# Attention with a gated output on one core: where a weight copy stands in ScalarE's order, and when placements and late fetches are issued

## Chip, core and metric

The kernel runs on one core of a Trainium2 chip. The metric is device time in microseconds of one execution. A core has five engines that run side by side, each through its own instructions in order: TensorE (PE, matmuls; PEld is its weight load), VectorE (DVE), ScalarE (ACT), GpSimd (POOL) and SyncE (SP). SP computes nothing here; it issues nearly all DMA transfers, one after the other, and a transfer that has to wait for something holds up all that stand behind it in SP's order. ScalarE and VectorE are in the same position: an instruction that waits holds those behind it.

## What is computed

The input x is (2, 1024, 512), all in float32. Cut to what matters:

```
xn = layernorm(x)
q, k, v = xn @ Wq.T + bq, xn @ Wk.T + bk, xn @ Wv.T + bv     # 32 heads of 16
s  = causal_softmax(q k^T / 4) v @ Wo.T + bo
g  = silu(xn @ W_base.T + b_base + routed_low_rank(xn))      # 8 experts, best 2
out = x + s * g
```

## The kernel before, in words

The 1024 tokens of a batch are two chunks of 512 (`c` is 0 or 1), the 32 heads four column blocks of 8 heads (`oc` is 0 to 3). A unit `(b, oc, c)` is the attention of one column block for one chunk of queries. `units` fixes the order of all units (line 466), `plan` cuts each into steps (line 1231). A step computes scores of some keys against the queries on PE (`scores`, line 1524, into two PSUM tiles `s`), takes the exponential of both on ScalarE (tiles `pt`, line 56 is the helper through which all VectorE and most ScalarE instructions are recorded), masks on GpSimd (line 1566), and multiplies with the values on PE one step later (`values`, line 1571, into `av`). The scores of a step need the two PSUM tiles back from the exponentials of the step before.

Into these steps all other work is filled (`fill`, line 1431), in an order that is fixed when the program is written, by a planner's own account of the engines: `act.free` and `ve.free` are the times at which ScalarE and VectorE are reckoned to be done, `begins` is when the next step starts. Three kinds of things are filled in. Tasks with a cost are PE work, cut to share the steps evenly. Tasks without a cost (layernorm, routing, weight sums) are run step by step on VectorE; they pause at a `WAIT` till the next step, and stop where `enough()` says that VectorE is late. `later` is a list of single pieces with the step from which they may be issued; a piece that has an entry in `costs` is put off while ScalarE is not `calm`, up to a last step. `urgent` is a list of DMA pieces that `place_urgent` (line 1519) issues: at the end of the tasks' turn in `fill`, and ahead of each step's scores.

Projections are done in seven block products in place of eight (sums of blocks of the weights and of the tokens are formed on VectorE first; `PARTS` names the seven). For the query and key columns of block `oc`, `qk_weights_task` (line 621) loads 0.5 MB of columns (`load_qk`, line 123), has ScalarE copy them so that the heads of a pair lie side by side (`pair_up`, line 129), forms four sums on VectorE, and stores the 1 MB result to HBM for the second batch (line 642), which fetches it again (line 626). Two buffers `wqk` serve all blocks. Blocks 0 and 1 are prepared elsewhere; the task's copy serves blocks 2 and 3. The weights of values, gate and output come in parts of 256 KB (`issue_parts`, line 617), four parts ahead of their use; those that are sums are read back from a stored copy `kept`.

A finished query or key block is split into high and low parts, and half of its rows are moved to other partitions by DMA before scores can use them: `place_keys` (line 465), `place_queries` (line 484, tile `qT`, 512 KB in two transfers). `split` puts them on the `urgent` list.

The output stage of a chunk (`out_task`, line 877) computes four blocks in the order (0,0), (1,1), (0,1), (1,0). For each, VectorE multiplies with the gate block `gr` and adds the input block `xr`, both fetched from HBM (lines 890 and 892) into two buffers each: the first two pairs are fetched at the start, the third and the fourth after (0,0) and (1,1) are done with theirs. The result is stored by line 903.

The attention's denominators go out by DMA (`den`, `dens`), are inverted, and come back (`back`, then `avs<-back`, line 1050).

Of the kernel before, what the change touches and what calls it, by code (L numbers as in the profile page):

```python
# [81 lines left out]
def direct(ctx, tc, sound, x, wq, wk, wv, wo, wb, wa, wg, wB, bq, bk, bv, bo, bb, out):  # L82
# [35 lines left out]
    def load_qk(oc):  # L118


        t = sb.tile([P, 4 * KC, P], F32, tag="wqk", bufs=2, name=f"wqk{oc}")
        for n, src in enumerate((wq, wk)):
            nc.sync.dma_start(
                out=t[:, (2 + n) * KC : (3 + n) * KC],
                in_=src.rearrange("(kc p) o -> p kc o", p=P)[:, :, oc * P : oc * P + P],
            )
        return t

    def pair_up(t):


        raw, paired = (
            t[:, i * KC : (i + 2) * KC].rearrange("p k o -> p (k o)") for i in (2, 0)
        )
        act.copy(
            paired.rearrange("p (g r a) -> p g a r", a=2, r=HD),
            raw.rearrange("p (g a r) -> p g a r", a=2, r=HD),
        )
# [15 lines left out]
    wqks = [load_qk(0)]  # L154
# [62 lines left out]
    WAIT = object()  # L217
    PAUSE = object()
    turned_at, now = {}, [0]
# [351 lines left out]
    def four_sums(at, to):  # L571

        ve.tensor_tensor(to[1], at[0, 1], at[0, 0], ALU.subtract)
        yield PAUSE
        ve.tensor_tensor(to[3], at[1, 1], at[0, 1], ALU.subtract)
        yield PAUSE
        ve.tensor_tensor(to[2], at[1, 1], to[1], ALU.subtract)
        yield PAUSE
        ve.tensor_tensor(to[4], at[1, 0], to[2], ALU.subtract)
# [41 lines left out]
    def qk_weights_task(n):  # L621

        oc = n % KC
        if n >= KC:
            wqks.append(sb.tile([P, 4 * KC, P], F32, tag="wqk", bufs=2, name=f"wqk{oc}"))
            nc.sync.dma_start(out=wqks[n], in_=qk_kept[oc])
        else:
            if n >= 2:
                wqks.append(load_qk(oc))
                for _ in range(3):  # L630
                    yield WAIT
                pair_up(wqks[n])
                yield WAIT
            w = wqks[n]
            yield from four_sums(
                {(i, j): w[:, 4 * j + 2 * i : 4 * j + 2 * i + 2] for i in range(2) for j in range(2)},
                {t: w[:, 2 * KC + 2 * t - 2 : 2 * KC + 2 * t] for t in range(1, 5)},
            )
            qk_kept[oc] = dram.tile([P, 4 * KC, P], F32, tag=f"kept_qk{oc}", bufs=1, name="kept")
            qk_ready[n] = now[0]  # L640
            yield WAIT
            nc.sync.dma_start(out=qk_kept[oc], in_=w)
            for _ in range(2):
                yield WAIT
        qk_ready.setdefault(n, now[0] + 2)
        yield WAIT
# [229 lines left out]
    def out_task(k):  # L876

        _, b, c = stages[k]
        y, g = block_of(chunk_tile(b, c)), block_of(g_tiles[b, c])
        order = [(0, 0), (1, 1), (0, 1), (1, 0)]  # L880
        xts, gts = {}, {}

        def block(t, i, j):
            rows = slice(c * C + BK * i, c * C + BK * i + BK)
            return t[b, rows, BK * j : BK * j + BK].rearrange("(t p) o -> p t o", p=P)

        def load():
            i, j = order[len(xts)]
            xts[i, j] = sb.tile([P, 2, BK], F32, tag="xr", name=f"xr_{b}_{c}_{i}{j}")
            nc.sync.dma_start(out=xts[i, j], in_=block(x, i, j))  # L890
            gts[i, j] = sb.tile([P, 2, BK], F32, tag="gr", name=f"gr_{b}_{c}_{i}{j}")
            nc.sync.dma_start(out=gts[i, j], in_=g(i, j))

        def final(i, j):
            def gated():
                ve.scalar_tensor_tensor(y(i, j), y(i, j), 0.5, gts[i, j], ALU.mult, ALU.mult)
                ve.tensor_tensor(y(i, j), y(i, j), xts[i, j], ALU.add)
                later.append((now[0] + 2, store))
                if i == j:
                    later.append((now[0] + 2 - i, load))  # L900

            def store():
                nc.sync.dma_start(out=block(out, i, j), in_=y(i, j))

            patient.append(gated)
            later.append((now[0], gated))

        load()
        load()
        yield from block_task(k, y, final)  # L910

    g_tiles = {}
# [175 lines left out]
    turns, turned, posts, posted, later, patient, last_out = [], [], {}, [], [], [], []  # L1088
# [16 lines left out]
    bases, whole_wo, splits, costs, urgent = {}, [], [], {}, []  # L1105
# [200 lines left out]
    for b in range(NB):  # L1306
        for c in range(NC):
# [69 lines left out]
            else:  # L1377
                before = starts[b, KC - 1, c] + 2
                Task(len(plan) - 7, bases_task(b, c), 0.0, after=before - 12, takes={"xnT": 2})
                n = len(units) - 3  # L1380
# [50 lines left out]
    def fill(n):  # L1431


        nonlocal spent
        now[0], begun_at = n, spent
        within = 0 <= n < len(plan)
        for x in tasks:
            x.waiting = False
        for turn in [turn for turn in turns if turn[0] <= n]:
            turns.remove(turn)  # L1440
            turn[1]()

        begin = len(plan) - 3
        even = (total - spent) / max(1, len(plan) - n)
        if n == len(plan) - 1:
            even = MM
        if n >= starts[units[-1]] - 8 and n < begin:
            even = sum(x.left for x in tasks if x.steps.__name__ not in ("whole_task", "rest_task"))
            even /= begin - n
        elif n < begin:  # L1450
            even = min(even, (total - last_work - spent) / (begin - n))
        share = spent + even
        if n >= 5:

            left = 0.0
            for x in tasks:
                if x.steps.__name__ in ("whole_task", "rest_task"):
                    continue
                left += x.left
                if x.due > n:  # L1460
                    share = max(share, spent + left / (x.due - n))
        while True:
            free = [x for x in tasks if x.cost and x.released(n)]
            if not free or free[0].due > n + 1:
                due = [x.steps.__name__ for x in tasks if x.cost and x.due <= n + 1]
                if due:
                    assert late, (n, due)
                    turn_late()
                    continue
                if not free or spent + (MM / 2 if n < 12 else MM / 8) >= share:  # L1470
                    break
            task = active[0] if active else free[0]
            active[:] = [task]
            ve.ready = act.ready = clock[0] + SV + spent - begun_at + MM
            cost = task.step()
            if cost is None or cost is WAIT:
                task.waiting = True
                active.clear()
            else:
                spent += cost  # L1480
        ve.ready = act.ready = 0.0
        begins = clock[0] + max(2.3, SV + spent - begun_at)
        enough = lambda more=0.65: late_by(n + 1, begins, more) > 0
        calm = lambda more: act.free + more < begins + 0.75
        for x in [x for x in splits if x[0] <= n]:
            if room["qT"] and room["kT"] and (calm(1.1) or n >= starts[x[2]] - 5):
                splits.remove(x)
                room["qT"] -= 1
                room["kT"] -= 1
                x[1]()  # L1490
        for x in [x for x in later if x[0] <= n]:
            if x not in later or x[0] == n and x[1] in patient and enough():
                continue
            if x[1] in costs and not calm(costs[x[1]][0]) and n < costs[x[1]][1]:
                continue
            later.remove(x)
            x[1]()
        for x in [x for x in tasks if not x.cost]:
            if not x.released(n):
                continue  # L1500
            said = PAUSE
            while said is not None and said is not WAIT:
                if x.due > n and enough(1.85 if x.due > n + 20 else 0.65):
                    break
                said = x.step()
            x.waiting = said is WAIT
        clock[0] = begins
        place_urgent(n)
        issue_parts()
        for _ in range(1 if active or len(plan) - 5 < n < len(plan) else 2):  # L1510
            if late and (min(x[0] for x in late) <= n or not within):
                turn_late()
# [6 lines left out]
    def place_urgent(n):  # L1519
        for x in [x for x in urgent if x[0] <= n]:  # L1520
            urgent.remove(x)
            x[1]()
# [124 lines left out]
    while late or turns or tasks:  # L1647
        fill(last + 99)
# [462 lines left out]
```

## Time and profile before

| what | value |
|---|---|
| median of 4 runs | 560.43 us (560.03 to 561.37) |
| the profiled execution, its time | 560.81 us |
| its span, first to last instruction | 559.0 us |
| mean granted TensorE clock | 0.994 |
| PE busy | 540.7 us of the span |
| ScalarE busy | 351.0 us |
| VectorE busy | 334.7 us |
| GpSimd busy | 118.5 us |
| share of the 16 DMA engines that the SP transfers took | 42.8% |
| longest total wait of SP: for PE to free a weight part (line 617) | 81.1 us in 35 waits |

How to read it: all times in a profile are of one execution, counted from the start of its span. A bracket behind an instruction gives the idle time of its engine just before it and what ended that time. PE at 97% means that nearly every other engine's idle time is free of cost; what counts is idle time of PE, and stretches in which the granted clock is below 1. The clock is the share of full speed at which PE was allowed to run. Time between a transfer's issue on SP and the instruction that waited for it is the transfer's latency; the DMA columns of a window tell how busy the 16 engines were with all transfers together.

### The profile page before, as it was taken

How to read it: one execution, taken by the hardware profiler on the slowest of the kernel's cores; microseconds unless marked ns; L12 is line 12 of the kernel's file. 1: busy time of each engine (PE TensorE's matmuls, PEld its weight loads, DVE VectorE, ACT ScalarE, POOL GpSimd, SP SyncE). 2: the span in 40 equal slices, each digit the busy share in tenths (PEclk: the TensorE clock that was granted, in tenths of full speed). 3: DMA queues.
4: the chain of work that ended last, by engine and by line, in shares of the span. 5: the costliest groups of instructions: out<-in, count | busy, mean ns of one | idle time of the engine just before them, and what ended most of it. 6: DMA issues, size and time to landing. Idle time of an engine off the chain costs nothing.

```text
span 559.0 us, 19432 instructions
## 1 busy us (share of the span) xinstructions
PE 540.7 (97%) x8411; PEld 280.1 (50%) x8411; DVE 334.7 (60%) x693; ACT 351.0 (63%) x389; POOL 118.5 (21%) x248
## 2 busy tenths in 40 slices
PE   8999999779999999999999999999999999999994
PEld 8435444444445554454645554444545554456651
DVE  4435587265478676466559765575267553648833
ACT  2537754655677766766667756656667777776540
POOL 2213401020213431130214330130103331020500
PEclk9999999998999999999999999999999999999998
DMA  8634370685624663732555545640124221652211
GB/s 262 173 112 172 119 232 1 211 301 179 168 77 137 226 221 113 233 112 73 185 167 174 175 155 161 205 153 23 58 80 137 79 83 45 227 171 81 97 40 45
DMA packets 65197, 79.15 MB, mean 142 GB/s; under 512 B 9560, under 2 KB 52576, under 8 KB 63696
## 3 DMA queue, kind: packets, MB, share of 16 engines
q1 hardware_dynamic: 65088, 77.83, 42.8%
q8 instruction: 68, 1.11, 0.9%
q14 instruction: 25, 0.20, 0.1%
q10 hardware_dynamic: 16, 0.00, 0.0%
HBM read 46.39 MB, written 19.37 MB: 118 GB/s over the span
## 4 chain that ended last, share of the span: by engine, by line
PE 89%; DVE 4%; DMA 3%; ACT 2%; issue 1%; SPq 0%; POOL 0%; ACTq 0%; POOLq 0%; DVEq 0%
PE av L1590 24%; PE p L228 22%; PE s L1538 17%; PE q L228 13%; PE pv L228 2%; PE po L228 2%; PE ph L228 2%; ACT pt L56 2%; PE pq L228 1%; PE pk L228 1%; DMA qT<-qT 1%; PE warm L183 1%; DVE x L56 1%; DMA wqk<-in_wk_dram 1%; DMA gr<-kept_g 1%
## 5 line engine op out<-in xcount | busy, mean ns | idle before, releaser
L56 ACT ACTIVATE pt<-s 128x1024 f32<-128x1024 f32 x288 | 290.0, 1024 | 157.0 <-PE s L1538 149.5
L1566 POOL TENSOR_SCALAR_AFFINE_SELECT pt<-pt 128x256 f32<-128x256 f32 (+1 forms) x224 | 110.5, 508 | 414.6 <-ACT pt L56 413.8
L1590 PE MATMUL av<-pt,v 128*32 128x512 f32 (+3 forms) x1680 | 156.9, 467 | 0.2 <-DVE v L56 0.2
L1538 PE MATMUL s<-qT,kT 32*128 32x512 f32 (+3 forms) x1616 | 108.8, 364 | 6.6 <-ACT pt L56 3.6
L1538 PEld LDWEIGHTS s<-qT,kT 32*128 32x128 f32 x1616 | 62.3, 183 | 65.9 <-issue 34.9
L1590 PEld LDWEIGHTS av<-pt,v 128*32 128x32 f32 x1680 | 41.6, 108 | 54.7 <-issue 38.6
L228 PE MATMUL p<-wt,asum 128*32 128x256 f32 x960 | 60.3, 387 | 0.0
L228 PE MATMUL q<-asum,wqk 128*32 128x256 f32 x832 | 51.2, 379 | 1.1 <-DVE qf L56 1.1
L228 PEld LDWEIGHTS p<-wt,asum 128*32 128x32 f32 x960 | 32.0, 112 | 29.7 <-issue 12.9
L228 PE MATMUL q<-xnT,wqk 128*32 128x256 f32 x624 | 39.5, 379 | 0.0
L228 PEld LDWEIGHTS q<-asum,wqk 128*32 128x32 f32 x832 | 26.5, 110 | 25.5 <-issue 7.2
L228 PEld LDWEIGHTS q<-xnT,wqk 128*32 128x32 f32 x624 | 20.2, 110 | 18.5 <-issue 6.6
L56 DVE TENSOR_TENSOR g<-p,g 128x512 f32<-128x512 f32 x20 | 13.8, 690 | 24.8 <-PE p L228 24.7
L56 DVE SCALAR_TENSOR_TENSOR kf<-q,kf 128x256 f32<-128x256 f32 x39 | 16.5, 424 | 19.5 <-PE q L228 18.6
L228 PE MATMUL p<-w,xnT 128*32 128x256 f32 x448 | 28.1, 379 | 0.0
L228 PEld LDWEIGHTS p<-w,xnT 128*32 128x32 f32 x448 | 15.7, 110 | 10.3 <-issue 3.6
L228 PE MATMUL p<-w,asum 128*32 128x256 f32 x320 | 20.7, 379 | 0.0
L56 DVE TENSOR_TENSOR kf<-kf,kT 128x512 f32<-128x512 f32 x15 | 10.3, 685 | 11.9 <-ACT kT L56 11.8
L228 PEld LDWEIGHTS ph<-wag_sb,xnT 128*32 128x32 f32 x512 | 15.2, 110 | 3.9 <-issue 3.3
L228 PE MATMUL po<-wo,oT 128*32 128x512 f32 x128 | 16.5, 593 | 0.4 <-ACT oT L56 0.4
L228 PE MATMUL ph<-wag_sb,xnT 128*32 128x136 f32 x512 | 16.6, 279 | 0.0
L56 DVE TENSOR_TENSOR v<-p,v 128x512 f32<-128x512 f32 x15 | 10.3, 684 | 10.5 <-PE p L228 10.4
(145 smaller groups left out, 557.8 us busy)
## 6 DMA issues: line engine op xcount, KB each, us to landing
wt<-kept SPq DMA_DIRECT2D x40, 256.0 KB
qT<-qT SPq DMA_DIRECT2D x30, 256.0 KB
x<-in_x_dram SPq DMA_DIRECT2D x16, 256.0 KB
kept<-wqk SPq DMA_DIRECT2D x4, 1024.0 KB
wqk<-kept SPq DMA_DIRECT2D x4, 1024.0 KB
kT<-kf SPq DMA_DIRECT2D x30, 128.0 KB
scr<-sq SPq DMA_DIRECT2D x6, 512.0 KB
xnT<-scr SPq DMA_DIRECT2D x24, 128.0 KB
```

Of the source, the lines that this page charges most:

```text
L56: return getattr(self.engine, name)(*args, **named)
L183: nc.tensor.matmul(warm[:, n % 4 * P : n % 4 * P + P], lhsT=ident, rhs=ident, start=True, stop=True)
L228: nc.tensor.matmul(o[j : j + 32], lhsT=lhsT[:, j : j + 32] if len(lhsT.shape) == 2 else lhsT[:, j // 32], rhs=rhs, start=start, stop=stop,)
L1538: nc.tensor.matmul(ss[s // 2][:, s % 2, col : col + w], lhsT=keys[rows, kt % TT * P : kt % TT * P + P], rhs=q[rows, halves * par + half_, ...
L1566: nc.gpsimd.affine_select(out=d, in_=d, compare_op=ALU.is_ge, fill=0.0, base=0, pattern=[[0, d.shape[1]], [1, P]], channel_multiplier=-1,)
L1590: nc.tensor.matmul(avs_now[par][32 * s : 32 * s + 32, q0 : q0 + w], lhsT=vs[b, kt][:, h * VS - HD * par : h * VS - HD * par + HP], rhs=pt[ ...
```

## The change

Three edits; the arithmetic and the number of instructions stay the same.

1. The pairing copy of blocks 2 and 3 is no longer issued by the task itself, three steps after the load. It becomes a piece of `later`, with a cost of 1.05 us of ScalarE: from the next step on it is issued when ScalarE is reckoned to have that much room, and at the latest four steps on. The task waits until it has been issued, and one step more, before it forms the sums.
2. In `fill`, `place_urgent` is called ahead of the tasks without a cost instead of behind them.
3. In the output stage, the late fetch is issued a step after its block in both cases (before: two steps after (0,0), one after (1,1)), and the multiplication of block (1,0) may be issued only from the next step.

```
@@ qk_weights_task
-                pair_up(wqks[n])
+                paired = lambda: pair_up(wqks[n])
+                costs[paired] = (1.05, now[0] + 4)
+                later.append((now[0] + 1, paired))
+                while any(x[1] is paired for x in later):
+                    yield WAIT
                 yield WAIT
@@ out_task, final
                 if i == j:
-                    later.append((now[0] + 2 - i, load))
+                    later.append((now[0] + 1, load))
...
             patient.append(gated)
-            later.append((now[0], gated))
+            later.append((now[0] + i * (1 - j), gated))
@@ fill
             later.remove(x)
             x[1]()
+        place_urgent(n)
         for x in [x for x in tasks if not x.cost]:
...
         clock[0] = begins
-        place_urgent(n)
         issue_parts()
```

Because the planner's account decides where pieces stand, the edits move more than they name. In the instruction lists of the two programs: on ScalarE the copy of block 2 moves to where the copy of block 3 stood, that one 16 instructions on, and a copy of the remainder of a query block moves ahead of two exponentials; on VectorE both groups of weight sums move later, as do the statistics, normalizing and transposes of the second batch's first layernorm and its token sums, and in two output stages token sums now stand ahead of a gated multiplication; on SP the load of block 3 and both stores of sums move later, placements of keys and queries stand ahead of them, the second transposed half of that layernorm is stored and read back later, and the late fetches of all three output stages stand ahead of stores and weight parts that they followed before. On PE and GpSimd only the cuts between neighbouring pieces of work differ.

More of the change, by code (lines that the diff above doesn't have):

```diff
@@ L631, in qk_weights_task @@
                     yield WAIT
-                pair_up(wqks[n])
+                paired = lambda: pair_up(wqks[n])
+                costs[paired] = (1.05, now[0] + 4)
+                later.append((now[0] + 1, paired))
+                while any(x[1] is paired for x in later):
+                    yield WAIT
                 yield WAIT
@@ L899, in gated @@
                 if i == j:
-                    later.append((now[0] + 2 - i, load))
+                    later.append((now[0] + 1, load))
             def store():
@@ L905, in final @@
             patient.append(gated)
-            later.append((now[0], gated))
+            later.append((now[0] + i * (1 - j), gated))
         load()
@@ L1497, in fill @@
             x[1]()
+        place_urgent(n)
         for x in [x for x in tasks if not x.cost]:
@@ L1507, in fill @@
         clock[0] = begins
-        place_urgent(n)
         issue_parts()
```

## The prediction

> **What bounds the kernel now.** I began with the page: its busy times, its slices, its chain.
>
> ```profile
> PE 540.7 (97%) x8411; PEld 280.1 (50%) x8411; DVE 334.7 (60%) x693; ACT 351.0 (63%) x389; POOL 118.5 (21%) x248
> ...
> PEclk9999999998999999999999999999999999999998
> ...
> PE 89%; DVE 4%; DMA 3%; ACT 2%; issue 1%; SPq 0%; POOL 0%; ACTq 0%; POOLq 0%; DVEq 0%
> ```
>
> TensorE is busy 540.7 of 559.0 us, so everything that any edit can win lies in 18.3 us of idle PE and in the one slice where the clock fell. The table of 10 us windows says where these are. Some 2.4 us stand ahead of 50 us and 8.3 us about the last matmuls, and the change touches neither. What is left is 0.60 + 3.08 + 2.83 between 90 and 130 us, 0.49 in 370 to 380 and 0.61 in 490 to 500.
>
> ```profile
> core 0: us, PE busy (x) PEld busy (x) DVE busy (x) ACT busy (x) POOL busy (x), PEclk, DMA share, GB/s
> ...
> 100.00:110.00 10.00, 6.92 (x140) 4.12 (x136) 0.69 (x1) 6.40 (x10) 0.00 (x0) 1.00 0.75 236
> 110.00:120.00 10.00, 10.00 (x172) 5.36 (x172) 5.47 (x12) 5.74 (x7) 2.86 (x6) 1.00 0.78 281
> 120.00:130.00 10.00, 7.17 (x92) 3.31 (x88) 7.84 (x26) 5.24 (x8) 1.27 (x2) 0.83 0.61 224
> ```
>
> The timeline of that stretch names the causes (columns: start, duration, engine, line, operation; in brackets the idle time before it and who ended it).
>
> ```profile
> 103.60 1.11 ACT L56 COPY wqk<-wqk 128x1024 f32<-128x1024 f32 x1 [3.77 <-DMA wqk<-in_wk_dram]
> ...
> 105.67 0.50 PE L1538 MATMUL s<-qT,kT 32*128 32x512 f32 x2 [2.66 <-ACT pt L56]
> ...
> 113.64 0.89 SPq L617 DMA_DIRECT2D wt<-kept  x2
> 114.58 0.46 SPq L123 DMA_DIRECT2D wqk<-in_wq_dram  x1
> ...
> 115.09 0.51 SPq L123 DMA_DIRECT2D wqk<-in_wk_dram  x1
> ...
> 115.64 1.16 SPq L465 DMA_DIRECT2D kT<-kf  x2
> ...
> 116.90 0.53 SPq L642 DMA_DIRECT2D kept<-wqk  x1
> ...
> 117.47 1.93 SPq L484 DMA_DIRECT2D qT<-qT  x2
> ...
> 124.03 0.73 PE L1538 MATMUL s<-qT,kT 32*128 32x512 f32 x8 [2.83 <-DMA qT<-qT]
> ```
>
> Two stalls follow each other. In the first, ScalarE comes to the pairing copy at 99.83 and stands there 3.77 us, because the columns (issued 98.62) land at 103.5; the exponentials queued behind it start at 104.61, so the next scores start at 105.67. In the second, the doubled queries qT are issued at 117.47, behind the next columns' load (0.5 MB) and the sums' store (1 MB), and land 6.42 us later at 123.89; the DMA engines are full from 115 to 125 us. In 1 us windows the granted clock is then 0.72, 0.50, 0.50, 0.57 from 125 to 129: 0.28 + 0.50 + 0.50 + 0.43 = 1.7 us more lost.
>
> **The change, part by part.** The instruction lists of the two programs, which hold no times, show what moves.
>
> *Pairing copy.* No instruction is added. The first copy (1.11 us) moves behind 14 ScalarE instructions, to the place where the second stood; the second (1.17 us) moves behind 16, to about 140 us. Neither then waits for its load: the first's columns have been there for 12 us. Removed: the 3.77 us stand at 99.83, and the 2.10 us one that the second copy had at 117.4. Without the first, the exponentials start 0.85 us after their scores (96.82 after 95.97 is the usual step), so 100.27 to 102.3, and PE goes on at 103.0 when its `ph` products end. The scores' following `av` stands at 107.24 now and would stand at 103.67: **3.57 us sooner**. ScalarE does not stall it again: two `hl` copies, keys (1.08) and exponentials (1.95) end at 106.3, PE wants the bank at 106.46.
>
> *What is late next.* SP doesn't move with PE here. From 98.62 to 113.64 it is held by its own order and by DMA: `back` lands at 108.5, the gate weights' 1 MB store at 113.59, and only then the two `wt` loads are issued, in both programs. PE now uses the first `wt` at 116.75 without waiting; 3.57 us sooner it asks at 113.18, and must wait. When does it land? Not after 116.75, as nothing waited then. Not before 115.9: the first bytes after the pause moved in the half microsecond from 114.5, and 256 KB at the 300 GB/s of that window take 0.85 us. I take the middle, **116.35**. So PE idles 3.2 us at a new place, and of the 3.57 us only 0.4 is left there (bounds 0 and 0.85). VectorE is no tighter: it frees the bank that this product needs at 113.7 (shuffle at 110.97, then 0.75 + 0.69 + 0.68 + 0.69, less overlap).
>
> *Placements.* After the two `wt`, SP's list now has kT, then qT at once; the load of the fourth columns comes four DMAs later, the sums' store ten. qT's issue moves from 117.47 to 113.64 + 0.89 + 1.16 + gaps = 115.72. The four column sums (1.97 us of VectorE ahead of qT's subtraction at 114.25) go too, so the ScalarE copy that SP waits for ends at 113.7 and holds nobody. Landing of qT: at least 115.72 + 2.35 = 118.1 (the small `avs<-back` took 2.35 from first issue); at most 115.72 + 6.42 = 122.14. A lone qT pair, issued at 163.95, had moved all its bytes by 167.0; here `wt` and kT (0.77 MB) are ahead and 1.5 MB less than before. I take 119.9. PE asks for it 4.45 us after the first `wt` product (116.75 to 121.20 now), at 116.35 + 4.45 = **120.8**, so it no longer waits. Gain over the whole stretch: 124.03 - 120.8 = **3.2 us**; bounds 2.8 (the `wt` at 116.75) and 3.9 (qT at 120), and 1.9 if qT keeps its 6.42.
>
> *The clock.* The row: after 2.83 us of idle PE it halved for 3.4 us, after 2.66 + 0.42 it did not. The new gap is 3.2 us, longer than either, so I leave the 1.7 us in the sum at its old price; the bounds are 0 and 1.7 us of gain. The Trainium skill, "TensorE: Matmul & The Clock Gate", section "HAM oscillation", warns of idle gaps above about 3.4 us, with a window that runs freely. By that rule neither old gap should have throttled, which the 2.83 us one did here; taken literally the new gap would escape and the estimate be 1.7 us lower.
>
> *Moved sums, loads, stores.* The first sums move to where the second stood (122.98, product at 145.3), the second to about 147 (product at 162.3); VectorE idles 2.11 us before the add at 149.66, which takes 1.74. Cost 0, hidden by 14 us or more. If that cover failed, one product would wait for up to 1.7 us. The 1 MB store lands behind `avs<-back` with no reader until the second batch.
>
> *Layernorm of the second batch.* VectorE's account shifts it later. Its last transposed tile was issued at 207.78; now it stands behind `avs<-back` (213.38 + 1.10): store 214.5, 3.1 to 4.0 us until the read may start (194.30 to 197.38, 203.79 to 207.78), 2.65 for four issues, some 2 for landing: 223.4 in the old times. Its first product is at 224.80. Cost 0, but only 1.4 us of cover.
>
> *Output stage.* The fetch of the third pair comes a step (3.4 us) sooner, ahead of a store and a weight load on SP, and the token sums stand ahead of the gated multiplication that waited for it.
>
> ```profile
> 373.04 0.69 DVE L56 SCALAR_TENSOR_TENSOR x<-x,gr 128x512 f32<-128x512 f32 x1 [2.16 <-DMA gr<-kept_g]
> ...
> 376.40 1.93 PE L228 MATMUL q<-asum,wqk 128*32 128x256 f32 x32 [0.49 <-DVE qf L56]
> ```
>
> That 0.49 us goes. The same edit in the other two output stages meets a PE without idle time: 0. Their weight load, now behind 0.5 MB, has three more tiles loaded ahead of it.
>
> **Sum.** 3.2 + 0.5 = 3.7 us off the profiled execution: 560.81 - 3.7 = 557.1 (span 559.0 to 555.3). The median of the four runs, 560.43, lies 0.38 lower, so I forecast **556.7**.
>
> **Rivals**, as times on that median.
> A. As above, the stalls merge into one at `wt` and the clock still dips once: 556.0 to 557.4. Chance 0.48.
> B. The clock stays up after the new gap: 556.7 - 1.7 = 555.0, to 554.4 if `wt` lands early. For: one old gap of 3.08 us did no harm. Against: the new one is longer and unbroken. 0.24.
> C. qT is late all the same: landing at 122.14 leaves 1.9 + 0.5 = 2.4, so 558.0, up to 559.2 if `wt` also holds. For: 6.42 us is the only latency seen here. Against: 1.5 MB fewer ahead of it. 0.12.
> D. The edits do not do what they say, or the gain is spent: VectorE adds the gate's product at 119.7 (0.68), then does the moved sums (1.74), the routing (2.05, as from 124.64 to 126.7 now) and the copy (0.68) that frees the `av` bank at 124.9; PE asks for it at 120.8 + 0.73 + 1.0 + 1.73 + 0.67 = 124.9. A slip of 3 us there leaves 559.3 to 561.6. 0.09.
> E. Slower: the layernorm's last tile. Each microsecond that it lands after 224.8 costs one, and it decides from 4.8 + 1.4 = 6.2 us beyond my reckoning. The longest waits of SP are of that size (6.2 us for VectorE, 4.2 for `back`); both in a row would cost 10.4 - 1.4 = 9.0 and give 565.7. Against: none of them stood there before. 0.07.
>
> **How the numbers follow.** A measurement of this kernel can tell about 0.2% (1.1 us) from no change, so "faster" is below 559.3: A, B and C, 0.84. D is the same, 0.09; E slower, 0.07. The range takes in A, B and C, 554.4 to 559.2.
>
> **What would show it.** Right: ScalarE's wait for `wqk` gone; PE without idle near 103 to 106 and with some 3 us before the first `p<-wt` near 113 to 116, put down to `wt<-kept`; SP issuing `wt` at 113.6 as before and qT near 115.7; scores after it near 120.8; no idle near 376. Wrong: SP's `wt` issue moved, qT still ended PE's wait, a PE gap near 220, or a `wt` that lands well before 115.9, which would make more of the 3.57 us real.

## The result, and the profile after

| | before | after |
|---|---|---|
| median | 560.28 us (78 runs) | 558.65 us (52 runs) |
| lowest to highest | 558.79 to 567.2 us | 554.68 to 561.68 us |
| span of the profiled execution | 559.0 us | 557.4 us |
| its mean granted clock | 0.994 | 0.990 |

The changed kernel is faster: ratio 0.9968, 95% interval 0.9959 to 0.9976, which is 1.8 us. The forecast was 556.7 us in a range of 554.4 to 559.2. The sign is right and the range holds the time, but the gain is half of the 3.7 us that were reckoned, and nearly all of it comes from another edit than the one that was to bring it.

First the page of the changed kernel: busy times, the granted clock in 40 slices, the shares of the chain of waits.

```profile
PE 540.8 (97%) x8411; PEld 280.6 (50%) x8411; DVE 333.0 (60%) x693; ACT 351.5 (63%) x389; POOL 116.2 (21%) x248
...
PEclk9999999979999999999999999999999999999998
...
PE 91%; DVE 2%; DMA 2%; ACT 1%; SPq 1%; issue 0%; POOL 0%; ACTq 0%; POOLq 0%; DVEq 0%
```

VectorE's share of the chain fell, and the clock has one deeper slice (7 in place of 8), still near 120 us. The 10 us windows show the same stretch.

```profile
100.00:110.00 10.00, 10.00 (x188) 5.61 (x192) 0.87 (x2) 8.62 (x12) 0.63 (x2) 1.00 0.77 239
110.00:120.00 10.00, 5.37 (x82) 2.57 (x72) 4.53 (x14) 3.60 (x5) 1.71 (x5) 0.81 0.57 217
120.00:130.00 10.00, 9.85 (x143) 4.89 (x140) 5.52 (x20) 5.32 (x6) 1.27 (x2) 0.84 0.60 183
```

PE's 3.08 us idle at the copy are gone (10.00 busy in 100 to 110) and so are the 2.83 us at qT. In their place stand 4.63 us between 110 and 120, and the clock is below 1 in two of these 10 us windows in place of one. PE is busy 25.22 us of these 30, before 24.09, in part only because it works longer at the lower clock. The timeline names the new wait.

```profile
104.19 0.93 SPq L1037 DMA_DIRECT2D back<-rc  x1
110.63 1.04 SPq L1054 DMA_DIRECT2D avs<-back  x2
111.77 0.39 SPq L597 DMA_DIRECT2D kept<-w_gate  x1
115.68 0.89 SPq L617 DMA_DIRECT2D wt<-kept  x2
...
117.87 1.23 SPq L484 DMA_DIRECT2D qT<-qT  x2
...
118.52 1.93 PE L228 MATMUL p<-wt,asum 128*32 128x256 f32 x16 [4.63 <-DMA wt<-kept]
...
125.02 0.74 PE L1542 MATMUL s<-qT,kT 32*128 32x512 f32 x8
```

The chain of waits (start, length, what) runs through three transfers:

```profile
104.19 6.39 DMA back<-rc
...
111.77 3.90 DMA kept<-w_gate
115.68 2.71 DMA wt<-kept
```

These transfers, 13 us in all, follow one upon the other: `back` must land before SP comes to `avs<-back`, that one stands ahead of the gate sums' store on SP, and the fetch of `wt` reads what that store wrote. PE arrives 3.5 us sooner at the end of a chain that does not arrive sooner.

Two stretches of PE hold the whole gain. The first runs from SP's load of block 2's columns (near 99 us) to the first `h` product (near 135), the second from the first `ph` product after 262 us to the first after 385. Each number is of one profiled execution.

| kernel | first stretch, us | second stretch, us |
|---|---|---|
| before | 37.16 | 124.55 |
| copy_alone | 35.97 | 124.21 |
| output_alone | 35.19 | 122.99 |
| output_gated_alone | 35.70 | 123.00 |
| output_fetch_alone | 36.15 | 124.27 |
| after | 36.22 | 123.02 |
| keep_warm | 36.96 | 122.99 |
| gate_store_first | 33.08 | 122.99 |
| gate_store_no_copy | 33.29 | 123.00 |
| columns_store_later | 31.83 | 122.98 |
| both_stores_moved | 29.92 | 122.99 |
| both_stores_no_copy | 36.57 | 123.02 |

From before to after the first stretch gives 0.94 us, the second 1.53; between them 0.36 is lost, and the start was 0.47 later in this execution: with 0.04 at the end that is the 1.6 us of the two spans. The second column splits cleanly by whether the gated multiplication was moved. The first scatters: before, output_alone, output_gated_alone and output_fetch_alone run the same program there and took 35.19 to 37.16, mean 36.05. The two with the copy moved and the stores in their old places, after and copy_alone, took 36.10 in the mean. In that order of stores the copy's new place is worth nothing that can be seen.

### The profile page after: what moved, and what is told of

Read it like the earlier page. It is cut to its first block, busy times and chain, and to the rows that moved or that the text cites. A ratio compares the mean times of both kernels' runs of the same rounds, so it can differ in the third digit from the quotient of the medians.

```text
span 557.4 us, 19435 instructions
## 1 busy us (share of the span) xinstructions
PE 540.8 (97%) x8411; PEld 280.6 (50%) x8411; DVE 333.0 (60%) x693; ACT 351.5 (63%) x389; POOL 116.2 (21%) x248
## 4 chain that ended last, share of the span: by engine, by line
PE 91%; DVE 2%; DMA 2%; ACT 1%; SPq 1%; issue 0%; POOL 0%; ACTq 0%; POOLq 0%; DVEq 0%
PE av L1594 25%; PE p L228 22%; PE s L1542 17%; PE q L228 14%; PE pv L228 2%; PE po L228 2%; PE ph L228 2%; PE pq L228 1%; PE pk L228 1%; DMA back<-rc 1%; ACT pt L56 1%; PE warm L183 1%; PE pq_first L351 1%; DMA kept<-w_gate 1%; DVE g L56 1%; PE h L228 1%
## 5 line engine op out<-in xcount | busy, mean ns | idle before, releaser
L1570 POOL TENSOR_SCALAR_AFFINE_SELECT pt<-pt 128x256 f32<-128x256 f32 (+1 forms) x224 | 108.2, 498 | 415.6 <-ACT pt L56 414.9
L56 DVE TENSOR_TENSOR x<-p,x 128x512 f32<-128x512 f32 x15 | 10.3, 687 | 10.3 <-PE p L228 10.2
L56 DVE TENSOR_TENSOR qT<-qf,qT 128x512 fp32r<-128x512 f32 x15 | 10.3, 685 | 9.8 <-ACT qT L56 9.8
```

The lines of the kernel that those rows point to most:

```text
L56: return getattr(self.engine, name)(*args, **named)
L1570: nc.gpsimd.affine_select(out=d, in_=d, compare_op=ALU.is_ge, fill=0.0, base=0, pattern=[[0, d.shape[1]], [1, P]], channel_multiplier=-1,)
```

## The experiments

Edit 2 by itself (`place_urgent` ahead of the tasks) was not run: in the instruction lists it changes the order on no engine, neither put into before nor left out of after, nor in any kernel below. The kernels below that leave out edit 1 leave out edit 2 with it. That leaves edits 1 and 3.

**The two edits apart.** copy_alone is before with edit 1, output_alone is before with edit 3.

```
copy_alone, on before                       output_alone, on before
-    pair_up(wqks[n])                       -  later.append((now[0] + 2 - i, load))
+    paired = lambda: pair_up(wqks[n])      +  later.append((now[0] + 1, load))
+    costs[paired] = (1.05, now[0] + 4)     -  later.append((now[0], gated))
+    later.append((now[0] + 1, paired))     +  later.append((now[0] + i * (1 - j), gated))
+    while any(x[1] is paired for x in later):
+        yield WAIT
```

> Only the first edit, on the kernel before. Theory 1 (the pairing copy carries the gain, and the wt load behind the denominators' return bounds it): 1.2 to 1.6 us below the kernel before, and the same new idle time of 3 to 5 us ahead of the first product with wt. Theory 2 (the output stage carries the gain, and the copy only exchanges one stall for another): within 0.5 us of the kernel before.

Measured: 560.14 against 560.39 us of before, ratio 0.9996 (0.9975 to 1.0017).

> Only the third edit, on the kernel before. Theory 1: the 0.49 us of idle PE near 376 goes and nothing else changes, 0.3 to 0.6 us below the kernel before. Theory 2: 1.3 us or more below it.

Measured: 558.71 against 560.39 us, ratio 0.9968 (0.9952 to 0.9984). The split is the reverse of the forecast's: the output stage brings the whole gain, 1.7 us, and the copy nothing on balance. My first theory fell here. The next question was what eats the 3.5 us that the copy does set free.

**The chain to `wt`, and the clock behind it.** In gate_store_first the gate sums' store is issued on SP ahead of `avs<-back`, so that it no longer waits for `back`; nothing else changes its order.

```
@@ the weight sums' task, on after
-        yield WAIT
-        nc.sync.dma_start(out=kept, in_=w)
-        combined[name], kept_at[name] = kept, now[0]
+        def store():
+            nc.sync.dma_start(out=kept, in_=w)
+            combined[name], kept_at[name] = kept, now[0]
+
+        if name == "gate":
+            urgent.append((now[0] + 1, store))
+            while name not in combined:
+                yield WAIT
+        else:
+            yield WAIT
+            store()
```

> The changed kernel, with the store of the gate's weight sums issued on SP ahead of the return of the denominators (avs from back), one step sooner, and nothing else. Theory 1: wt is then issued some 3 us sooner, the 4.63 us wait ahead of its first product falls to 1 to 2 us, and the clock does not dip: 4 to 6 us below the changed kernel, 553 to 555 us. Rival (what holds the product is the DMA engines' load and not SP's order): the wt lands no sooner, since the 1 MB store then stands in the busy time, and the time stays within 1 us of the changed kernel.

Measured: 555.79 us, ratio 0.9906 (0.9879 to 0.9933), 2.9 us below after, where 4 to 6 were expected. `wt` is issued 3 us sooner, and the wait left over is another one:

```profile
112.70 0.89 SPq L625 DMA_DIRECT2D wt<-kept  x2
...
115.62 1.68 PE L228 MATMUL p<-wt,asum 128*32 128x256 f32 x16 [2.03 <-DVE g L56]
```

This product also needs the PSUM bank that VectorE frees by its additions to `g`, and these stand on VectorE behind the shuffle `rb<-avs`, which waits for `avs<-back`. `back` holds PE by two ways.

keep_warm puts 56 products without use ahead of the first product with `wt` in after (their result is overwritten by the products that follow), to keep the clock up while PE waits. On PE they are 112 matmuls, two for each product: the page counts 8523 in place of 8411.

```
@@ the products of a stage, on after
+            if stages[k] == ("gate", 0, 0) and name == "p6":
+                for _ in range(14):
+                    matmul(ps[:, 0:BK], lhsT=a[:, 0, 0:P], rhs=a[:, 1], start=True, stop=True)
```

> The changed kernel, with 56 more matmuls of 128x256 (3.0 us) ahead of the first product with wt, into the same PSUM tile, which that product then overwrites; the stall stays, PE only is not idle in it. If the dip of the clock costs what the 1 us windows say, the time falls by 1.7 to 2.4 us against the changed kernel. If the dip costs nothing because PE waits for other things anyway, it stays within 0.5 us; if the matmuls outlast the wait, it rises by up to 1 us.

Measured: 560.11 us, ratio 0.999 (0.9975 to 1.0006). The clock stayed at 1.00 throughout the stretch, but the added work took 6.1 us, twice the 3.0 that were reckoned for it, and outlasted the wait that it was to fill:

```profile
115.72 6.25 PE L228 MATMUL p<-asum 128*32 128x256 f32 x112 [1.54 <-DVE g L56]
121.79 1.05 PE L228 MATMUL p<-wt,asum 128*32 128x256 f32 x16
```

So this is no way to gain, but it prices the time at half clock: from the first `wt` product to the first `h` product it took 14.67 us with the clock up and 16.79 us in after, 2.1 us (one execution of each).

**The other store of the chain, and the copy with a short chain.** `back` itself stands behind 1 MB: SP issues the store of block 0's column sums right ahead of it. columns_store_later issues that store four steps on, behind the gate store, ahead of `wt`. both_stores_moved does this and gate_store_first's edit together; there the fetch of `wt` goes ahead of the column store. gate_store_no_copy and both_stores_no_copy are gate_store_first and both_stores_moved without edit 1.

```
@@ qk_weights_task, on after (both_stores_moved: with the diff above too)
-            nc.sync.dma_start(out=qk_kept[oc], in_=w)
+            def store():
+                nc.sync.dma_start(out=qk_kept[oc], in_=w)
+            if n == 0:
+                later.append((now[0] + 4, store))
+            else:
+                store()
```

> The changed kernel, with one store moved: the 1 MB of column sums of block 0 (`kept<-wqk`, L646), which SyncE issues at 103.2 us ahead of the second `back` load, is issued four steps later, right ahead of the fetch of `wt`. Theory (the copy's 3.6 us are taken back by the chain `back` (6.4 us from issue to landing), gate sums' store, fetch of `wt`): `back` has no megabyte ahead of it and lands in 2 to 4 us instead of 6.4, the gate sums' store leaves 2 to 4 us sooner, the wait ahead of the first product with `wt` falls from 4.63 to 1 to 3 us, and the time is 2 to 4 us below the changed kernel's: 554.5 to 556.5. Rival (what is short is the DMA engines' time, so the moved megabyte only stands ahead of `wt` instead): the wait stays within 1 us of 4.63, the time within 1 us of 558.65.

Measured: 557.52 us (554.6 to 560.49), ratio 0.9947 (0.9925 to 0.9969), 1.1 us below after. In its profile, whose time of 554.8 us is among its lowest:

```profile
103.16 0.41 SPq L1044 DMA_DIRECT2D back<-rc  x1
106.21 1.04 SPq L1061 DMA_DIRECT2D avs<-back  x2
...
111.30 1.56 SPq L617 DMA_DIRECT2D wt<-kept  x2
...
115.97 1.07 PE L228 MATMUL p<-wt,asum 128*32 128x256 f32 x16 [2.46 <-DVE key L56]
```

From `back` to `avs<-back` it takes 3.05 us in place of 6.44: the megabyte ahead of it costs `back` 3.4 us. But it now stands right ahead of `wt`. The bracket names `key`, an instruction of VectorE's routing; the addition to `g` that ended this product's wait in gate_store_first was over at 111.54 here, so what PE waits for is most likely `wt` itself, 4.67 us from its issue in place of 2.71. To that extent the rival is right.

The median is above what was expected, and the clock of its runs fits a reason. Four had a clock of 0.995 or 0.996 and a median of 555.0 us, four of 0.991 or 0.992 and 557.5, four of 0.989 or 0.990 and 559.3. The profiled one, of 0.995, has no time at half clock in this stretch. The others may differ by whether a wait that is left starts such a time; each step of the clock costs 1.8 to 2.5 us. This is read from the clock alone, as only one execution was profiled.

> The changed kernel with both stores moved: that of the gate's weight sums ahead of the stores that wait for `back`, and that of block 0's column sums behind the fetches of `wt`. Theory of the chain: `wt` is issued before 112 us and has landed when TensorE comes to it, the wait ahead of the first product with it falls under 1 us, the half-clock windows behind it go too, and the time is 4 to 6.5 us below the changed kernel's: 552 to 554.5. Rival (DMA time is short): no better than with the gate store alone moved, 555.79 within 0.7 us.

Measured: 553.23 us, ratio 0.9868 (0.9846 to 0.989), 5.4 us below after and 6.9 below before, the fastest kernel of this study. All its six runs have a clock of 0.995 to 0.997. TensorE comes to `wt` and finds it there:

```profile
109.25 0.89 SPq L625 DMA_DIRECT2D wt<-kept  x2
...
112.97 1.05 PE L228 MATMUL p<-wt,asum 128*32 128x256 f32 x16
...
118.34 0.74 PE L1557 MATMUL s<-qT,kT 32*128 32x512 f32 x8 [0.92 <-DMA qT<-qT]
```

That the DMA engines lack time was the rival, and here it fell: the same bytes move, only in another order.

> gate_store_first without the part of the change that places the copy: block 0's pairing copy stands where it stood before, all else is as in gate_store_first (555.79). It tells what the copy is worth once the fetch behind it comes sooner. Theory (the copy's gain is real, and in the changed kernel the chain to `wt` takes it back): without the copy it is 1.5 to 3 us slower, 557.3 to 558.8. Rival (the copy's place is worth nothing in any order, and the gate store's gain is its own): 555.79 within 0.7 us.

Measured: 557.98 us, ratio 0.9947 (0.993 to 0.9965): without the copy's new place 2.2 us slower than gate_store_first. Here the profiles do not repeat the medians: the first stretch took 33.29 against 33.08 us. The profiled execution without the copy was that kernel's fastest of nine, 556.01 us.

> both_stores_moved without the part of the change that places the copy. Theory: with the fetches early the copy's whole stand of 3.6 us is to be seen, so this is 2.5 to 4 us slower than both_stores_moved, 555 to 558. Rival (the copy is worth nothing in any order): within 0.7 us of both_stores_moved.

Measured: 558.79 us, ratio 0.9969 (0.9953 to 0.9984): 5.6 us slower than both_stores_moved. This is more than the copy's stand, since the stand is also followed by time at half clock:

```profile
106.61 2.13 PE L1553 MATMUL s<-qT,kT 32*128 32x512 f32 x8 [2.89 <-ACT pt L56]
...
106.60:113.30 6.70, 6.57 (x60) 3.35 (x64) 3.46 (x8) 4.92 (x8) 0.00 (x0) 0.50 0.56 200
```

2.89 us idle, and 6.70 us at a clock of 0.50, of which half is lost: 6.2 us, where the first stretches differ by 6.65. And it is no faster than output_alone (558.71), which has neither store moved: without the copy's new place the two stores bring nothing, as the copy's place brings nothing without them.

So edit 1 is worth 0.25 us in the order of stores of before, which is not to be told from nothing, 2.2 us with one store moved, 5.6 us with both. Its gain is real; in the changed kernel the chain takes it back. The 2.2 us compare runs of two sessions; the ratios against before in the same session (0.9906 and 0.9947) give 2.3.

**The output stage, in two.** output_gated_alone is before with the moved due time of the gated multiplication alone (that of the fourth block; the second keeps its own), output_fetch_alone with that of the fetches alone.

> The kernel before, with one of the two edits of the output stage: the due time of the gated multiplication of the second and fourth block moved by one step, the fetches left where they stood. Theory (the gain of the output stage is VectorE's queue order: at 373 us of before the gated multiplication waits 2.16 us for `gr`, and the sums `asum` and the differences `qf`, `kf` behind it make TensorE, ScalarE and the products `q` late): all or nearly all of output_alone's gain, 1.2 to 1.7 us below before, 558.5 to 559. Rival (the fetches issued sooner bring it): within 0.4 us of before, 559.8 to 560.5.

Measured: 559.63 against 560.21 us, ratio 0.9984 (0.9965 to 1.0003): by time alone this cannot be told from no change.

> The kernel before, with the other edit of the output stage alone: the late fetches of `xr` and `gr` due one step sooner, the gated multiplications left where they stood. Theory (queue order of VectorE): the multiplication still stands ahead of the sums; where `gr` lands sooner its wait of 2.16 us shrinks, but the two multiplications still take their 1.4 us ahead of the sums, so 0 to 0.6 us below before, 559.6 to 560.2. Rival (the fetches bring the gain): 1.2 to 1.7 us below before.

Measured: 560.52 against 560.21 us, ratio 1.0009 (0.9985 to 1.0034). The times leave the split open; the traces give it. With the multiplication moved the second stretch took 123.00 us, as much as with both (122.99); with the fetches alone 124.27, 0.28 less than before, which is no more than copy_alone (124.21), a kernel with neither. All nine kernels with the multiplication moved took 122.98 to 123.02 us here, the three others 124.21 to 124.55. Between the two stretches and behind the second, output_gated_alone and output_alone agree to 0.03 us, so the 0.9 us between their medians most likely come from the first 134 us, in which the two run the same program; but by the medians a part for the fetches is not excluded. VectorE's rows in output_gated_alone:

```profile
368.97 0.68 DVE L56 TENSOR_TENSOR asum<-asum,xnT 128x512 f32<-128x512 f32 x1
369.56 0.69 DVE L56 TENSOR_TENSOR asum<-xnT,asum 128x512 f32<-128x512 f32 x1
...
372.35 0.68 DVE L56 SCALAR_TENSOR_TENSOR x<-x,gr 128x512 f32<-128x512 f32 x1
```

The sums now go first and the multiplication finds `gr` landed. In output_fetch_alone it still stands ahead of the sums and still waits, as before:

```profile
372.11 0.69 DVE L56 SCALAR_TENSOR_TENSOR x<-x,gr 128x512 f32<-128x512 f32 x1 [1.70 <-DMA gr<-kept_g]
```

## Why the prediction was right or wrong

**The range holds the time by luck.** copy_alone, which has the edit that was to bring 3.2 us, took 560.14 us; less the 0.5 that the output stage was to bring, this is 559.6, above the range. What brought the time into it is 1 us more from the output stage.

**The copy's stand: right.** ScalarE no longer waits for `wqk`. The `av` that was to stand at 103.67 stands at 104.07, less the 0.47 us by which this execution started later: 103.60.

**"SP doesn't move with PE here": the step that failed.** The place was right (a new wait at the first product with `wt`, ended by `wt<-kept`), the size was not. `wt` was to be issued at 113.64 and its first part to land at 116.35. It was issued at 115.68, or 115.21 in the times of before, 1.57 us late; from issue to landing it took 2.71 us, just what had been taken. All of the delay lies ahead of `avs<-back`: `back` was issued 0.16 us later, and SP came to `avs<-back` 6.44 us after it in place of 5.03. From there to `wt` both kernels took 5.05 us. It is no accident of one execution: with the column store in its old place the four programs with edit 1 took 6.44, 6.36, 6.51 and 5.89 us, the five without it 5.03, 4.70, 5.20, 5.45 and 5.16. I had taken a transfer's latency for a fixed one because nothing of SP's order ahead of it moved.

VectorE's bank, reckoned free at 113.7, came free at 115.3 (115.75 less the shift), for the same cause. Had `wt` been there, PE would still have waited some 2 us, as gate_store_first shows (2.03).

**The clock: mis-sized.** It was left in at its old price of 1.7 us. With the longer wait the clock was at half for about 7 us in place of 3.4, and PE ran through 4.7 us of them:

```profile
113.00:118.50 5.50, 0.89 (x20) 0.27 (x9) 3.51 (x8) 3.31 (x4) 1.53 (x4) 0.80 0.66 252
118.50:123.20 4.70, 4.68 (x51) 2.36 (x54) 1.15 (x6) 1.31 (x3) 0.40 (x1) 0.51 0.97 313
```

That is 2.3 us, and keep_warm measures 2.1. The two errors account for the stretch: scores after qT were forecast at 120.8; `wt` 1.7 us late (118.05 in the times of before against 116.35) and 2.3 us of half clock make 124.8; they stood at 124.55, where before had 124.03 (its own time at half clock came behind these scores). The upper bound of the gain, 3.9 us, does not follow from its terms either: a `wt` at 115.9 and 4.45 us more are 120.35, which gives 3.7.

**qT: right.** It stands behind the `wt` and kT, the scores on it wait for nothing, and rival C, which gave nearly the measured time, gave it for a reason that did not happen. Rival B, the clock staying up at 555.0, would fit one of the 52 runs: 554.68 us, at a clock of 0.996. It was not profiled.

**The moved sums, loads and stores: right,** no wait of PE stands there. **The layernorm of the second batch:** no wait near 220 either, but the stretch from `h` to `ph` takes 0.36 us more in after and 0.37 more in copy_alone. PE's filled-in work is cut differently there, and one step's scores, which follow only 16 filled-in matmuls where before has 32, took 1.17 us (at 221.67) in place of 0.80. That the layernorm's shift is the cause was not tried.

**The output stage: mis-sized, 0.49 against 1.53 us.** The mechanism was right. But I read only the idle time of PE in front of one row. In before the step of scores that begins at 373.70 ran to 378.26:

```profile
373.70 0.74 PE L1538 MATMUL s<-qT,kT 32*128 32x256 f32 x16
374.37 1.54 PE L1590 MATMUL av<-pt,v 128*32 128x384 f32 x16
376.40 1.93 PE L228 MATMUL q<-asum,wqk 128*32 128x256 f32 x32 [0.49 <-DVE qf L56]
378.26 0.74 PE L1538 MATMUL s<-qT,kT 32*128 32x512 f32 x8
```

In after:

```profile
373.24 0.74 PE L1542 MATMUL s<-qT,kT 32*128 32x256 f32 x16
373.91 1.07 PE L1594 MATMUL av<-pt,v 128*32 128x384 f32 x16
374.80 1.91 PE L228 MATMUL q<-asum,wqk 128*32 128x256 f32 x32
376.64 0.74 PE L1542 MATMUL s<-qT,kT 32*128 32x512 f32 x8
```

It took 4.56 us in before and 3.40 in after. The 1.16 us too many are 0.49 of idle, and the rest is time that the page counts as busy: the same 16 `av` products took 1.54 us in before and 1.07 after. Another 0.4 us came near 302, which I had put at 0 because PE had no idle time there, and by another way: before has 16 filled-in matmuls between two steps' scores there, and the second scores took 1.16 us; after has 32, and they took 0.80. So it is the cut of PE's work, as near 221, and not VectorE's order.

## What to carry to other kernels

When a stall is taken away, follow the engine to its next wait and then follow that wait back through the whole chain that feeds it: here `back`, a store, a fetch, each behind the other on one queue, and once the copy had moved, moving two stores in that queue brought more (5.4 us) than the whole change had (1.8). Neither shows a gain alone: with the copy in its old place the same two stores brought nothing. Whether an edit is worth anything may be settled by the order of its neighbours: the same moved copy brought 0.25, 2.2 or 5.6 us. And the cost of a late operand is not only the idle time in front of a row: compare the step's length with that of its neighbours.

## What the runs showed of the hardware

**The length of a wait does not settle whether the clock falls.** In the profiled executions, PE's clock halved after 1.54 + 0.41 us of idle (gate_store_no_copy), 2.08 + 0.41 (output_alone), 2.53 + 0.41 (output_fetch_alone) and 2.03 (gate_store_first), each time for 3 to 4 us, and for about 7 us after 2.89 (both_stores_no_copy) and 4.63 (after). It did not fall after 2.66 + 0.42 (before) or 2.46 (columns_store_later). The four kernels that run the same program in the first stretch show it best: output_alone and output_fetch_alone halved the clock after the wait at the copy, before after the wait for qT, output_gated_alone not at all. The Trainium skill, "TensorE: Matmul & The Clock Gate", section "HAM oscillation", gives as its rule that there be no idle gaps above about 3.4 us; here gaps far below that throttled, and the measurement decides.

**Instructions are fetched through the same DMA engines.** Why `back` lands later in the programs with edit 1 was not settled by a run. The traces show one thing that differs. Of the transfers from 108.5 to 110 us in after:

```profile
q8 instruction: 1, 0.02, 3.9%
q1 hardware_dynamic: 30, 0.01, 3.7%
```

One 16 KB packet of instructions is moved here from 108.57 us on; it took 0.93 us. The last nine small packets of `back` begin at 109.49, as it ends, when all the others were over by 108.98. It is the same in every program with edit 1 and the column store in its old place: the nine begin at 109.04 in copy_alone, 109.43 in keep_warm and 109.26 in gate_store_first, within 0.02 us of the end of an instruction packet. In before, output_alone, output_fetch_alone and gate_store_no_copy `back` was complete before the packet began; in output_gated_alone the packet began earlier, at 107.44, and `back` was complete at 108.27, ahead of its end. So the packet seems to hold up one part of `back`, by 0.6 to 1.2 us, and with this the issue of `avs<-back`. The copy lets PE run 3.5 us ahead, so it may ask for its instructions earlier. That this is the cause fits all these traces, but no run here moved the fetch by itself.
